# Cross-attention on one core: value products in five passes instead of six, with copies, loads and reciprocals rearranged

## The chip, the cores and the metric

The kernel runs on one core of a Trainium2 chip. The metric is device time in microseconds (us) of one execution; the time before is the median of three runs. The profile is of one further execution, so sums made from it are compared with its own time. Engine names are those of the profile: PE (TensorE), ACT (ScalarE), DVE (VectorE), POOL (GpSimd), SP (the queue that issues nearly all transfers).

## The reference

Only the text part of the attention counts here: the context has 77 rows, so the slices for objects, others and image prompts, which start at row 77, are empty and add nothing.

```python
# x: (32, 512, 640), ctx: (32, 77, 1024), 20 heads of 32 columns
q = heads(x @ to_q_w)
k = heads(ctx @ to_k_w)
v = heads(ctx @ to_v_w)
p = softmax(q @ k^T / sqrt(32))
out = merge(p @ v)
out = out @ to_out_w + to_out_b + x
```

## The kernel before

**Precision.** All products are made from split operands. A float32 value is split into a high part (rounded to the type float32r by a copy, mostly on ACT) and a low part (the value less its high part, mostly on DVE or POOL), and a product of two split operands is three matmuls: high x high, high x low, low x high (`PAIRS`).

**Stages.** First keys and values of all 32 batches are made from the context and written to scratch memory in DRAM (`k_dram`, `v_dram`). Then come 160 *slots*, one for each batch b and each chunk j of 128 columns (four heads): n = 5b + j. The order of every engine's queue is the order in which the program is written (a manual schedule), so each engine works its list in order and waits where an operand is missing.

**A slot n** holds several chunks at different ages:

- `queries(n + 1)` makes the next chunk's queries from the transposed, split x (15 matmuls of 512 columns in two parts, L437); `split_q` splits them (L103, L104).
- `scores(n, t)` for four quarters t: three matmuls of 308 columns (L456) and DVE's maximum per head (L464); `exps(n, t)` exponentiates four heads on ACT and sums them (L474).
- `sums(n - 1)` and `normalize(n - 1, ..)`: reciprocals on DVE (L484), one product on POOL (L489). `transpose_p(n - 1)` turns 32 x 32 blocks on DVE (L496) and writes the probabilities, transposed, to DRAM as 320 rows (10 blocks of 32 keys, three padding keys a head) of 512 queries (L503).
- `load_p` loads an older chunk's rows (L512, L513) into `raw`: 128 rows for each of two pairs of heads in planes 0 and 1, and the other 64 rows in half of plane 2. The probabilities of chunk n - 3 are then split: `cast_p` makes the high parts (ACT, L520), `rest_p` casts the rest rows (ACT, L526) and makes the low parts of planes 0 and 1 (DVE, L527), `last_p` makes the low parts of the rest rows (POOL, L534). The rest rows' high parts lie in partitions 0 to 63 of plane 4 of `pp` and their low parts in partitions 64 to 127.
- `values` multiplies them with the values in `vb` (L548): six matmuls of 512 columns, three for each pair p (high plane, low plane, plane 4), into two PSUM banks `pa`. A value block has its high part in the first 64 columns of a matmul's weights and its low part in the last 64, so high x high is in PSUM's partitions 0 to 63 and the product with the low part in 64 to 127.
- `sum_a` copies partitions 64 to 127 away (ACT, L559) and adds the halves (DVE, L561); `high_a` and `low_a` split the result (ACT L568, DVE L573).
- `piece` does part of the output projection of an earlier batch (L591); `finish` adds residual and bias (DVE, L620) and stores; `add_bias` prepares that sum on POOL (L584).
- For the next batch, `transpose_x` turns x (DVE, L256) in chunks 0 to 2, and `split_x` splits it in the slots of chunks 2 (two splits) and 3 (three): ACT L263, POOL L264.
- `refill` loads the next keys (L418) and values (L426): group 0 holds chunks 0 and 1, group 1 chunks 2 to 4. One half is issued at the start of the slot, the other after `load_p`. Group 1's keys load in chunk 0's slot, group 0's values in chunk 1's, group 0's keys in chunk 2's, group 1's values in chunk 3's.

**The order within a slot**, as far as the change touches it: first half of `refill`, `cast_p`, `high_a` of the chunk taken one slot earlier, `scores(n, 0)`, `rest_p`, `sums`, `last_p`, `normalize`, `low_a`, `exps(n, 0)`, the first queries, `scores(n, 1)`, `load_p`, the second half of `refill`, and so on; `values` and `sum_a` come late in the slot. The tiles `pp` and `pa` exist once each.

Of the kernel before, what the change touches and what calls it, by code (L numbers as in the profile page):

```python
# [23 lines left out]
P = 128  # L24
# [12 lines left out]
    (0, 0, 0, 0, 0, 80),  # L37
    (0, 0, 80, 1, 0, 48),
    (0, 1, 0, 1, 48, 32),
    (0, 1, 64, 1, 48, 32),  # L40
    (1, 0, 48, 3, 0, 80),
    (1, 0, 0, 2, 32, 48),
    (1, 1, 32, 2, 0, 32),
    (1, 1, 96, 2, 0, 32),
]

# [5 lines left out]
def kernel(  # L52
# [340 lines left out]
    raws, pps, ats, pds, sms, pqs, pas, xrs, pos = ({} for _ in range(9))  # L393
# [14 lines left out]
    for g, (j0, nj) in enumerate(GROUPS):  # L408
        vb = main.tile([P, nj, 2, 2, P], FPR, name=f"vb{g}")
        nc.gpsimd.memset(vb.bitcast(F32), 0.0)  # L410
        vbs.append(vb)
# [8 lines left out]
    def load_values(b, g, segments=SEGMENTS):  # L420
        j0, nj = GROUPS[g]
        v = v_dram.rearrange("n i j a d -> n j i (a d)")
        for p, t, r0, i, k0, kn in segments:
            k0 += b * NKEY
            c0 = i % 2 * HD
            nc.sync.dma_start(  # L426
                vbs[g][r0 : r0 + kn, :, p, t, c0 : c0 + 3 * HD].bitcast(F32),
                v[k0 : k0 + kn, j0 : j0 + nj, i, :].bitcast(F32),
            )
# [79 lines left out]
    def load_p(n):  # L509
        pd = pds.pop(n)  # L510
        raw = late[0].tile([P, 3, S], F32, tag="raw", name="raw", bufs=2)
        nc.sync.dma_start(raw[:, 0:2, :], pd.rearrange("(k p) q -> p k q", k=2)[:P])  # L512
        nc.sync.dma_start(raw[:64, 2, :], pd[P : P + 64, :])  # L513
        raws[n] = raw

    def cast_p(n):

        raw = raws[n]
        pp = late[0].tile([P, 5, S], FPR, tag="pp", name="pp", bufs=1)
        nc.scalar.copy(pp[:, 0:2, :], raw[:, 0:2, :])  # L520
        pps[n] = pp

    def rest_p(n):

        raw, pp = raws[n], pps[n]
        nc.scalar.copy(pp[:64, 4, :], raw[:64, 2, :])  # L526
        nc.vector.tensor_tensor(  # L527
            pp[:, 2:4, :], raw[:, 0:2, :], pp[:, 0:2, :].bitcast(F32), ALU.subtract
        )

    def last_p(n):

        raw, pp = raws.pop(n), pps[n]
        nc.gpsimd.tensor_tensor(  # L534
            pp[64:, 4, :], raw[:64, 2, :], pp[:64, 4, :].bitcast(F32), ALU.subtract
        )

    PASSES = [(p, 0, p + c) for p in range(2) for c in (0, 2)] + [(p, 1, 4) for p in range(2)]  # L540

    def values(n):
        b, j = divmod(n, NC_)
        g = GROUP_OF[j]
        pp, vb = pps.pop(n), vbs[g][:, j - GROUPS[g][0]]
        pas[n] = late[1].tile([P, 2, S], F32, tag="pa", name="pa", bufs=1)
        for m, (p, t, c) in enumerate(PASSES):
            nc.tensor.matmul(  # L548
                pas[n][:, p, :],
                vb[:, p, t, :],  # L550
                pp[:, c, :],
                start=(c == p),
                stop=(t == 1),
            )

# [88 lines left out]
    def take(m):  # L644
        values(m)
        sum_a(m)
        high_a(m)
        low_a(m)

    def refill(b, j, part):  # L650

        heads = range(2 * part, 2 * part + 2)
        segments = SEGMENTS[4 * part : 4 * part + 4]
        if j == 0:
            load_keys(b, 1, heads)
        elif j == 1:
            load_values(b, 0, segments)
# [5 lines left out]
    def slot(n, beside=()):  # L663
# [105 lines left out]
    def end():  # L769
# [6 lines left out]
        high_a(N - 4)  # L776
        cast_p(N - 3)
        low_a(N - 4)
# [11 lines left out]
        piece(last - 1, 9)  # L790
        cast_p(N - 2)
# [25 lines left out]
        take(N - 2)  # L817
        cast_p(N - 1)
# [4 lines left out]
        begin(2, 0, 3)  # L823
# [5 lines left out]
        begin(4, 0, 4)  # L829
        begin(5, 0, 4)  # L830
# [78 lines left out]
```

## Time and profile before

| | |
|---|---|
| median of three runs | 1937.06 us (1936.06 to 1937.77) |
| profiled execution | 1935.38 us, span 1933.3 us |
| granted clock of TensorE | 0.998 |
| busy | PE 98%, ACT 79%, DVE 74%, POOL 52% |
| transfers | 431.28 MB, 560919 packets |

A group of the profile names the line, the engine, the operation, output and inputs with their shapes, the count, then the busy time and the mean duration, then the idle time of the engine in front of these instructions and what ended it. A line of the timeline has the start in us from the start of the span, the duration, the engine, the line and the operation; instructions of one kind in a row are merged (x6), and their duration runs from the first start to the last end. Durations of matmuls include the way through the array, so that matmuls in a row overlap; their pitch is less than their duration.

### The profile page before, as it was taken

The numbers are of one execution on the slowest core, as the hardware profiler recorded it, in microseconds if no ns is written. First come the engines' busy times: TensorE is split into PE (matmuls) and PEld (weight loads), VectorE is DVE, ScalarE is ACT, GpSimd is POOL, SyncE is SP. The second block draws the span as 40 slices with busy tenths as digits, with TensorE's granted clock in tenths as the row PEclk, the third lists the DMA queues.
The fourth block names the chain that finished last, engine by engine and source line by source line (L and its number), as shares of the span: only waits on it lengthen the run. The fifth ranks groups of instructions, "written<-read, shape, count | busy, mean of one in ns | idle before, by whom it ended". The sixth has DMA issues, their size and how long they took to land.

```text
span 1933.3 us, 36251 instructions
## 1 busy us (share of the span) xinstructions
PE 1900.7 (98%) x10332; PEld 1696.9 (88%) x10332; DVE 1439.4 (74%) x2334; ACT 1532.6 (79%) x6210; POOL 1013.8 (52%) x668
## 2 busy tenths in 40 slices
PE   9999998999999999999999999999999999999998
PEld 7888896889999999999889998999989998988987
DVE  4444447788888888888788888887888888788875
ACT  3232248888998889888888888889899988888883
POOL 1100054656665566555556555566566656655654
PEclk9999999999999999999999999999999999999999
DMA  9888878888888888888889888888898888888875
GB/s 184 201 196 248 198 195 218 226 229 237 228 224 230 226 227 230 228 241 218 232 230 235 230 224 232 238 232 219 232 238 227 223 228 222 226 227 240 234 198 171
DMA packets 560919, 431.28 MB, mean 223 GB/s; under 512 B 187024, under 2 KB 469072, under 8 KB 560720
## 3 DMA queue, kind: packets, MB, share of 16 engines
q1 hardware_dynamic: 556208, 414.46, 82.8%
q0 software_dynamic: 4416, 14.34, 2.2%
q8 instruction: 84, 1.38, 0.3%
q14 instruction: 115, 0.94, 0.2%
q10 hardware_dynamic: 96, 0.16, 0.0%
HBM read 247.17 MB, written 181.64 MB: 222 GB/s over the span
## 4 chain that ended last, share of the span: by engine, by line
PE 33%; DMA 17%; ACT 16%; DVE 11%; POOL 10%; issue 10%; SPq 3%; DVEq 0%; POOLq 0%; ACTq 0%
PE po L591 8%; PE pq L437 8%; ACT pn L474 7%; DMA raw<-pd 7%; POOL pn L489 7%; PE pv L191 6%; DMA pd<-z 6%; PE pk L191 5%; PE sc L456 4%; POOL pp L534 3%; PE pa L548 3%; ACT xt L263 3%; DVE pp L527 2%; ACT aw L559 2%; DVE nm L464 2%
## 5 line engine op out<-in xcount | busy, mean ns | idle before, releaser
L474 ACT ACTIVATE pn<-sc,nm 128x77 f32<-128x77 f32 x2560 | 800.6, 333 | 65.7 <-DVE nm L464 62.8
L591 PE MATMUL po<-wo_s,at 128*128 128x320 f32 x3840 | 622.8, 310 | 10.2 <-DVE xr L620 6.5
L437 PE MATMUL pq<-xt,wq_s 128*128 128x512 f32 x2400 | 607.2, 393 | 0.6 <-POOL xt L264 0.6
L591 PEld LDWEIGHTS po<-wo_s,at 128*128 128x128 f32 x3840 | 573.9, 188 | 20.1 <-DVE xr L620 17.0
L534 POOL TENSOR_TENSOR pp<-raw,pp 64x512 fp32r<-64x512 f32 x160 | 211.1, 1319 | 647.5 <-ACT pp L526 402.2
L474 ACT ACTIVATION_READ_ACCUMULATOR pn<-sc,nm 128x1 f32 x2560 | 543.7, 212 | 0.0
L437 PEld LDWEIGHTS pq<-xt,wq_s 128*128 128x128 f32 x2400 | 436.9, 188 | 76.8 <-POOL xt L264 1.7
L456 PE MATMUL sc<-kb,qt 128*128 128x308 f32 x1920 | 378.8, 306 | 12.8 <-ACT pn L474 5.9
L456 PEld LDWEIGHTS sc<-kb,qt 128*128 128x128 f32 x1920 | 325.1, 189 | 58.5 <-ACT pn L474 9.4
L489 POOL TENSOR_TENSOR pn<-pn,rs 128x1232 f32<-128x1232 f32 x160 | 364.1, 2276 | 12.6 <-DVE rs L484 0.2
L496 DVE STREAM_TRANSPOSE z<-pn 128x1280 f32<-128x1280 f32 x160 | 241.8, 1512 | 161.1 <-POOL pn L489 152.9
L464 DVE TENSOR_REDUCE nm<-sc 128x4 f32<-128x308 f32 x640 | 295.4, 463 | 54.8 <-PE sc L456 51.6
L527 DVE TENSOR_TENSOR pp<-raw,pp 128x1024 fp32r<-128x1024 f32 x160 | 195.5, 1222 | 82.5 <-ACT pp L520 71.4
L548 PE MATMUL pa<-pp,vb 128*128 128x512 f32 x960 | 252.2, 398 | 1.6 <-DVE pp L527 0.8
L561 DVE TENSOR_TENSOR pa<-pa,aw 64x512 f32<-64x512 f32 x320 | 222.7, 696 | 27.9 <-ACT aw L559 18.7
L559 ACT COPY aw<-pa 64x1024 f32<-64x1024 f32 x160 | 161.8, 1011 | 79.6 <-PE pa L548 77.4
L264 POOL TENSOR_TENSOR xt<-xs,xt 128x512 fp32r<-128x512 f32 x160 | 203.9, 1293 | 38.0 <-ACT xt L263 37.5
L548 PEld LDWEIGHTS pa<-pp,vb 128*128 128x128 f32 x960 | 174.8, 189 | 32.0 <-DVE pp L527 1.1
L584 POOL TENSOR_TENSOR xr<-xr,bias 128x640 f32<-128x640 f32 x128 | 201.3, 1574 | 0.2
L520 ACT CAST pp<-raw 128x1024 fp32r<-128x1024 f32 x160 | 168.8, 1055 | 31.9 <-DMA raw<-pd 31.8
L191 PE MATMUL pk<-ct,wk_s 128*128 128x512 f32 (+1 forms) x600 | 134.5, 382 | 1.4 <-ACT wk_s L103 1.1
L191 PE MATMUL pv<-ct,wv_s 128*128 128x512 f32 (+1 forms) x600 | 133.9, 382 | 0.0
(43 smaller groups left out, 1337.4 us busy)
## 6 DMA issues: line engine op xcount, KB each, us to landing
pd<-z SPq DMA_DIRECT2D x640, 160.0 KB, 3.8
raw<-pd SPq DMA_DIRECT2D x160, 512.0 KB, 4.0
xs<-in_x_dram SPq DMA_DIRECT2D x128, 320.0 KB, 6.2
xr<-in_x_dram SPq DMA_DIRECT2D x128, 320.0 KB, 4.0
out_dram<-xr SPq DMA_DIRECT2D x127, 320.0 KB, 4.0
raw<-pd SPq DMA_DIRECT2D x160, 128.0 KB, 4.2
v_dram<-vs SPq DMA_DIRECT2D x80, 192.0 KB, 4.0
k_dram<-ks POOLq DMA_DIRECT2D x20, 512.0 KB, 4.4
```

The source lines that it names most:

```text
L191: nc.tensor.matmul(held[j][:, :gn], w[:, k, a, :], cts[g, k][:, c, :gn], start=(k == 0 and n == 0), stop=(k == NK - 1 and n == 2),)
L437: nc.tensor.matmul(pqs[n], wq_s[:, k, a, j * P : (j + 1) * P], xts[b, k][:, c, :], start=(k == 0 and m == 0), stop=(k == NC_ - 1 and m == 2),)
L456: nc.tensor.matmul(sc[:, :KCOLS], qt[:, a, t * P : (t + 1) * P], kb[:, j - GROUPS[g][0], c], start=(m == 0), stop=(m == 2),)
L464: nc.vector.tensor_reduce(nm, sc[:, :KCOLS].rearrange("p (h k) -> p h k", k=NKEY), AX.X, ALU.max, negate=True)
L474: nc.scalar.activation(pnb[n % 2][:, at, :NKEY], sc[:, i * NKEY : (i + 1) * NKEY], AF.Exp, bias=nm[:, i : i + 1], accum_out=sms[n][:, at : ...
L489: nc.gpsimd.tensor_tensor(pf, pf, rs.unsqueeze(2).to_broadcast([P, NQ * HPC, NKEY]), ALU.mult)
L496: nc.vector.transpose(z.rearrange("p b t j -> p t b j"), pn.rearrange("p (t h) k -> p t (h k)", t=NQ).rearrange("p t (b i) -> p t b i", i=Q),)
L527: nc.vector.tensor_tensor(pp[:, 2:4, :], raw[:, 0:2, :], pp[:, 0:2, :].bitcast(F32), ALU.subtract)
L534: nc.gpsimd.tensor_tensor(pp[64:, 4, :], raw[:64, 2, :], pp[:64, 4, :].bitcast(F32), ALU.subtract)
L548: nc.tensor.matmul(pas[n][:, p, :], vb[:, p, t, :], pp[:, c, :], start=(c == p), stop=(t == 1),)
L561: nc.vector.tensor_tensor(pa[64 * p : 64 * p + 64, 0], pa[:64, p], aw[:, p], ALU.add)
L591: nc.tensor.matmul(pos[b, t, h][:, :HALF], ats[b * NC_ + j][:, a, t * P : (t + 1) * P], wos[0][:, j, c, h * HALF : (h + 1) * HALF], start= ...
```

## The change

- **Five passes.** The rest rows now lie twice in partitions 96 to 127: planes 0 and 1 hold rows 0 to 127 of each pair of heads, plane 2 the rows 96 to 159 of each (64 rows of either pair, so 32 of each lie in two places). The low parts of planes 0 and 1 are made for 96 partitions only, and the remaining 32 partitions of the two low planes take high parts of the rest rows, copied by POOL from plane 2. So two high passes and two passes over these mixed planes cover all but the low parts of the rest rows, and a fifth matmul, `rest_values`, multiplies those from a tile of their own (`lp`), made by POOL from all 128 partitions of plane 2.
- **Where it runs.** `rest_values` adds into `pa` after `sum_a` has added the halves there, in the next slot, behind the first queries; `high_a` and `low_a` follow behind `scores(n, 1)`.
- **Weights.** `vb` has five blocks per chunk. Three loads for each half of the heads (six, before eight) fill the first four; a new `copy_values` on POOL, in the slots of chunks 1 and 4, copies the rest.
- **Loads.** `load_p` has a second load of 64 rows. Group 0's values now load in chunk 0's slot and group 1's keys in chunk 1's.
- **Order.** One cast on ACT of all three planes; `sums` and `normalize` now stand in front of `rest_p` and `last_p`.

```diff
 SEGMENTS = [
-    (0, 0, 0, 0, 0, 80),
...
+    (0, 0, 0, 0, 80),
+    (0, 80, 1, 0, 48),
+    (2, 96, 1, 48, 32),
+    (1, 0, 2, 0, 80),
+    (1, 80, 3, 0, 48),
+    (3, 96, 3, 48, 32),
 ]
+REST = [(0, 0, 32), (32, 2, 32), (64, 1, 96), (96, 3, 96)]
...
-        vb = main.tile([P, nj, 2, 2, P], FPR, name=f"vb{g}")
+        vb = main.tile([P, nj, 5, P], FPR, name=f"vb{g}")
...
+    def copy_values(g):
+        vb = vbs[g]
+        nc.gpsimd.tensor_copy(vb[:96, :, 2:4, :], vb[:96, :, 0:2, :])
+        for r0, m, c0 in REST:
+            nc.gpsimd.tensor_copy(
+                vb[r0 : r0 + Q, :, 4, c0 : c0 + HD], vb[96:, :, m, HD : 2 * HD]
+            )
...
     def load_p(n):
-        nc.sync.dma_start(raw[:, 0:2, :], pd.rearrange("(k p) q -> p k q", k=2)[:P])
-        nc.sync.dma_start(raw[:64, 2, :], pd[P : P + 64, :])
+        rows = pd[: NBLK * Q].rearrange("(k p) q -> k p q", k=2)
+        nc.sync.dma_start(raw[:, 0:2, :], rows[:, :P].rearrange("k p q -> p k q"))
+        for k in range(2):
+            nc.sync.dma_start(raw[64 * k : 64 * k + 64, 2, :], rows[k, 96:])
...
     def cast_p(n):
-        nc.scalar.copy(pp[:, 0:2, :], raw[:, 0:2, :])
+        nc.scalar.copy(pp[:, 0:3, :], raws[n])
...
     def rest_p(n):
-        nc.scalar.copy(pp[:64, 4, :], raw[:64, 2, :])
         nc.vector.tensor_tensor(
-            pp[:, 2:4, :], raw[:, 0:2, :], pp[:, 0:2, :].bitcast(F32), ALU.subtract
+            pp[:96, 3:5, :], raw[:96, 0:2, :], pp[:96, 0:2, :].bitcast(F32), ALU.subtract
         )
     def last_p(n):
-        nc.gpsimd.tensor_tensor(
-            pp[64:, 4, :], raw[:64, 2, :], pp[:64, 4, :].bitcast(F32), ALU.subtract
-        )
+        nc.gpsimd.tensor_copy(pp[96:, 3, :], pp[32:64, 2, :])
+        nc.gpsimd.tensor_copy(pp[96:, 4, :], pp[96:, 2, :])
+        lp = late[0].tile([P, S], FPR, tag="lp", name="lp", bufs=1)
+        nc.gpsimd.tensor_tensor(lp, raw[:, 2, :], pp[:, 2, :].bitcast(F32), ALU.subtract)
+        lps[n] = lp
     def values(n):
-        for m, (p, t, c) in enumerate(PASSES):
+        for m, c in ((0, 0), (1, 1), (2, 3), (3, 4)):
             nc.tensor.matmul(
-                pas[n][:, p, :], vb[:, p, t, :], pp[:, c, :], start=(c == p), stop=(t == 1),
+                pas[n][:, m % 2, :], vbs[g][:, j - GROUPS[g][0], m, :], pp[:, c, :],
+                start=m < 2, stop=m > 1,
             )
+    def rest_values(n):
+        nc.tensor.matmul(
+            pas[n][:, 0, :], vbs[g][:, j - GROUPS[g][0], 4, :], lps.pop(n),
+            start=False, stop=True, skip_group_check=True,
+        )
...
     def refill(b, j, part):
         if j == 0:
+            load_values(b, 0, segments)
+        elif j == 1:
             load_keys(b, 1, heads)
-        elif j == 1:
-            load_values(b, 0, segments)
...
     def slot(n, beside=()):
             cast_p(taken)
-        if n - 1 in takes:
-            high_a(takes[n - 1])
         s = scores(n, 0)
+        if n:
+            normalize(n - 1, sums(n - 1))
         if taken is not None:
             rest_p(taken)
-        rs = sums(n - 1) if n else None
         if taken is not None:
             last_p(taken)
-        if n:
-            normalize(n - 1, rs)
-        if n - 1 in takes:
-            low_a(takes[n - 1])
+        if j in (1, 4):
+            copy_values(j // 4)
         exps(n, 0, *s)
         if ahead:
             queries(n + 1, 0, 2)
+        if n - 1 in takes:
+            rest_values(takes[n - 1])
         s = scores(n, 1)
+        if n - 1 in takes:
+            taken_parts(takes[n - 1], rest=False)
```

`taken_parts` calls `rest_values` (if asked), `high_a` and `low_a`. The last slots, written out one by one in `end`, get the same calls in the same sense.

More of the change, by code (lines that the diff above doesn't have):

```diff
@@ L391 @@
     late = []
-    raws, pps, ats, pds, sms, pqs, pas, xrs, pos = ({} for _ in range(9))
+    raws, pps, lps, ats, pds, sms, pqs, pas, xrs, pos = ({} for _ in range(10))
     bias = main.tile([P, C], F32, name="bias")
@@ L422, in load_values @@
         v = v_dram.rearrange("n i j a d -> n j i (a d)")
-        for p, t, r0, i, k0, kn in segments:
+        for m, r0, i, k0, kn in segments:
             k0 += b * NKEY
@@ L646, in take, with taken_parts @@
         sum_a(m)
+    def taken_parts(m, rest=True):
+        if rest:
+            rest_values(m)
         high_a(m)
@@ L817, in end @@
         take(N - 2)
+        begin(2, 0, 3)
+        taken_parts(N - 2)
         cast_p(N - 1)
@@ L829, in end @@
         begin(4, 0, 4)
+        taken_parts(N - 1)
         begin(5, 0, 4)
```

36 lines of the change are left out of this document (17 added, 19 removed).

## The prediction

> **What bounds the kernel now.** I read the page's busy times and groups first, then the stretches of five consecutive slots, then the timeline of those slots, the groups with shapes kept apart, the DMA issues and the waits. Page and groups (busy, mean ns of one, idle before):
>
> ```profile
> span 1933.3 us, 36251 instructions
> PE 1900.7 (98%) x10332; PEld 1696.9 (88%) x10332; DVE 1439.4 (74%) x2334; ACT 1532.6 (79%) x6210; POOL 1013.8 (52%) x668
> ...
> L534 POOL TENSOR_TENSOR pp<-raw,pp 64x512 fp32r<-64x512 f32 x160 | 211.1, 1319 | 647.5 <-ACT pp L526 402.2
> L489 POOL TENSOR_TENSOR pn<-pn,rs 128x1232 f32<-128x1232 f32 x160 | 364.1, 2276 | 12.6 <-DVE rs L484 0.2
> L527 DVE TENSOR_TENSOR pp<-raw,pp 128x1024 fp32r<-128x1024 f32 x160 | 195.5, 1222 | 82.5 <-ACT pp L520 71.4
> L264 POOL TENSOR_TENSOR xt<-xs,xt 128x512 fp32r<-128x512 f32 x160 | 203.9, 1293 | 38.0 <-ACT xt L263 37.5
> L584 POOL TENSOR_TENSOR xr<-xr,bias 128x640 f32<-128x640 f32 x128 | 201.3, 1574 | 0.2
> L520 ACT CAST pp<-raw 128x1024 fp32r<-128x1024 f32 x160 | 168.8, 1055 | 31.9 <-DMA raw<-pd 31.8
> ```
>
> PE is busy 98%. The stretches show that this is the bound of each slot: the five lines are chunks 1, 2, 3, 4 of one batch and chunk 0 of the next; columns are length, then PE, PEld, DVE, ACT, POOL busy, clock, DMA share, GB/s.
>
> ```profile
> 990.57:1000.67 10.10, 10.10 (x60) 9.17 (x59) 8.49 (x15) 7.98 (x34) 3.56 (x2) 1.00 0.77 228
> 1000.67:1010.77 10.10, 10.10 (x59) 9.18 (x58) 9.07 (x15) 9.40 (x39) 6.78 (x5) 1.00 0.77 206
> 1010.77:1020.85 10.08, 10.08 (x60) 9.17 (x58) 7.93 (x14) 9.86 (x40) 7.95 (x6) 1.00 0.88 239
> 1020.85:1030.93 10.08, 10.08 (x60) 9.16 (x59) 7.42 (x14) 9.05 (x42) 6.95 (x5) 1.00 0.84 190
> 1030.93:1041.36 10.43, 10.33 (x60) 9.16 (x59) 8.26 (x14) 9.13 (x42) 5.10 (x3) 1.00 1.12 282
> sum 50.79, PE 50.69 PEld 45.84 DVE 41.18 ACT 45.42 POOL 30.34; mean PE 10.14 PEld 9.17 DVE 8.24 ACT 9.08 POOL 6.07
> ```
>
> PE has no gap in four of five slots, at full clock. So a matmul less is worth its full pitch, and whatever makes PE wait is lost for good. The in-order queues of the other engines decide which it is. Their places:
>
> ```profile
> 1001.23 1.05 ACT L520 CAST pp<-raw 128x1024 fp32r<-128x1024 f32 x1
> ...
> 1002.49 0.46 DVE L464 TENSOR_REDUCE nm<-sc 128x4 f32<-128x308 f32 x1
> ...
> 1007.17 1.57 PE L548 MATMUL pa<-pp,vb 128*128 128x512 f32 x6
> ...
> 1011.20 1.55 PE L437 MATMUL pq<-xt,wq_s 128*128 128x512 f32 x6
> ...
> 1011.61 1.05 ACT L520 CAST pp<-raw 128x1024 fp32r<-128x1024 f32 x1
> ...
> 1013.01 2.23 PE L437 MATMUL pq<-xt,wq_s 128*128 128x512 f32 x9
> ...
> 1015.51 1.05 PE L591 MATMUL po<-wo_s,at 128*128 128x320 f32 x6
> ...
> 1016.40 1.55 PE L548 MATMUL pa<-pp,vb 128*128 128x512 f32 x6
> ...
> 1018.90 0.65 DVE L104 TENSOR_TENSOR qt<-pq,qt 128x512 fp32r<-128x512 f32 x1
> 1018.92 3.79 POOL L264 TENSOR_TENSOR xt<-xs,xt 128x512 fp32r<-128x512 f32 x3
> ...
> 1021.91 1.06 ACT L520 CAST pp<-raw 128x1024 fp32r<-128x1024 f32 x1
> ...
> 1027.35 1.56 PE L548 MATMUL pa<-pp,vb 128*128 128x512 f32 x6
> ...
> 1031.49 1.06 ACT L520 CAST pp<-raw 128x1024 fp32r<-128x1024 f32 x1
> ...
> 1032.00 0.46 DVE L464 TENSOR_REDUCE nm<-sc 128x4 f32<-128x308 f32 x1
> ...
> 1039.24 2.27 PE L591 MATMUL po<-wo_s,at 128*128 128x320 f32 x12
> ...
> 1039.84 0.48 DVE L620 TENSOR_TENSOR xr<-po,xr 128x320 f32<-128x320 f32 x1
> ```
>
> **The matmul removed.** Nine matmuls of 512 columns take 2.23 us and six 1.55, so one more costs (2.23 - 1.55)/3 = 0.227 us. Five passes for six: 160 x 0.227 = 36.3 us, 1.13 us a batch. If PE stays the only bound, the profiled execution (1935.4 us, span 1933.3; 1.7 under the median of 1937.1) becomes 1899.
>
> **The rest, engine by engine.**
>
> ```profile
> L526 ACT CAST pp<-raw 64x512 fp32r<-64x512 f32 x160 | 100.2, 626 | 0.0
> ...
> L104 DVE TENSOR_TENSOR qt<-pq,qt 128x512 fp32r<-128x512 f32 x160 | 104.6, 654 | 4.9 <-ACT qt L103 4.9
> ...
> L410 POOL MEMSET vb<- 128x1536 f32 x1 | 1.4, 1381 | 5.3 <-DMA k_dram<-ks 5.3
> ...
> L410 POOL MEMSET vb<- 128x1024 f32 x1 | 1.0, 952 | 0.0
> ```
>
> ACT: one cast of 1536 elements for casts of 1024 and 512. The slope is (1055 - 626)/512 = 0.84 ns, so it takes 1.48 us against 1.68: 0.2 us a slot less on an engine that isn't the bound; nothing. But the low parts (DVE L527) now wait for all 1.48 us, not 1.05.
>
> DVE: the subtract has 96 partitions and still 1024 elements: 1.22 us. The reciprocal only changes place.
>
> POOL: no such copy is in the trace. Below is the memset: slope (1381 - 952)/512 = 0.84 ns, so 0.52 us for 512 elements; above is the subtract L534, 1.32 in the mean. A copy reads one operand, not two, so I take 0.6, nearer the memset. Two a slot, and copy_values twice a batch at some 1.3 us (512 or 768 elements and four short ones). The subtract into the tile lp takes the 1.29 of the xt subtract L264, which has its shape. Per batch POOL goes from 30.3 us to 30.3 + 5 x 1.2 + 2 x 1.3 = 38.9 of 49.7: busier, not full.
>
> DMA: 160 x 128 KB more of raw, 21 of 431 MB; the values save 64 of 384 rows. Shares of 0.77 to 0.88 allow that. Only chunk 0's slot stands at 1.12, and there raw lands later; the next slot has ACT 7.98 busy of 10.10, which covers a cast that starts 1 to 2 us later. I cost it at nothing.
>
> **Moved.** The fifth pass runs one slot later, behind PE's first six query matmuls, and PE's whole queue stands behind it. They start 0.43 into the slot (1011.20), so it comes at 0.43 + 6 x 0.227 = 1.8. It needs lp, which POOL leaves in the slot before, and DVE's sum of the halves, which is done when the maximum of chunk 2's slot starts (1002.49, 1.82 into it), the latest of these: 0.1 there, nothing elsewhere. The high and low parts of a come behind it. In chunk 3's slot PE's projection reads them from 4.74 + 0.23 = 5.0 (high) and 5.3 (low); ACT's high part ends about 2.3 + 1.2 + 0.6 = 4.1, DVE's low part 0.9 to 1.1 behind the low parts of the probabilities: met, if those end by 4.2. The sums reuse one PSUM tile, so the passes also need that low part before 5.9 (6.7 in the other slots): met too. The values of group 0 now load in chunk 0's slot, a slot sooner, and copy_values reads them a slot later; both have a whole slot to land.
>
> **The order on POOL and DVE, on which the sign hangs.** Before, POOL's normalization follows DVE's low parts and never meets them. After, the reciprocal is ahead of the low parts, POOL starts its 2.28 us as soon as that is done, while DVE still waits for the 1.48 us cast. What do they do to each other when they meet? In the first slot with values there is one such meeting, DVE first, with an undisturbed subtract of a later slot below it:
>
> ```profile
> 299.83 1.22 DVE L527 TENSOR_TENSOR pp<-raw,pp 128x1024 fp32r<-128x1024 f32 x1 [1.95 <-ACT pp L520]
> ```
> ```profile
> 300.43 1.75 POOL L534 TENSOR_TENSOR pp<-raw,pp 64x512 fp32r<-64x512 f32 x1 [4.85 <-ACT pp L526]
> ```
> ```profile
> 1013.79 1.29 POOL L534 TENSOR_TENSOR pp<-raw,pp 64x512 fp32r<-64x512 f32 x1 [2.06 <-DMA pd<-z]
> ```
>
> POOL started 0.62 us before DVE's subtract ended and took 1.75 us, not 1.29: it stood still for 0.46 of the 0.62. So POOL doesn't run beside this DVE subtract. Whether DVE stands still when POOL was first, no row shows. The bounds are 0 and the rest of POOL's instruction, up to 2.28 us; nearest is the mirror image just shown, so I take the whole rest. The Trainium skill (SBUF — State Buffer, Who interferes with whom) says that a DVE instruction with two SBUF inputs and a GpSimd one that reads SBUF exclude each other, whoever starts first holding the port for its whole instruction. By that rule the sum is the one below, and for DVE first this trace agrees (1.75 against 1.29).
>
> The sum then goes by slots, in us from each slot's start, slots 0.23 shorter:
> - Chunk 2 (1000.67): the maximum ends at 2.28, the reciprocal at 2.5, the cast at 2.04. DVE is first, 2.45 to 3.67; POOL normalizes to 5.8, copies to 7.0. The passes would start at 6.73 and want the copied rows at 7.19: no stall but the 0.1 above. Then POOL's 1.29, 1.57 and two of 1.29 run to 12.5, 2.6 into the next slot.
> - Chunk 3 (1010.77): cast done at 2.32, POOL holds the port to 2.6, DVE's low parts end at 3.8, normalization at 6.0, copies at 6.6 and 7.2. The passes start at 5.86 here and want the copies at 6.32 and 6.55: PE waits 0.6. POOL ends 3.5 into the next slot.
> - Chunk 4 (1020.85): cast done at 2.54, port free at 3.5, low parts to 4.7, normalization to 6.9, copies to 8.1; wanted at 7.4: PE waits 0.7.
> - Chunk 0 (1030.93): the maximum ends at 1.53, normalization runs 1.85 to 4.13; the cast is done at 2.04, so the low parts run 4.13 to 5.35, 2.5 later than before. DVE's steps behind them (maximum, low a, maximum, transpose, low q, maximum, starting 0.38, 0.55, 0.38, 1.44, 0.57, 0.38 apart) put the end of L620 at 9.45, was 9.39. PE already waits for it there (2.27 for 12 matmuls, 1.92 elsewhere) and comes 0.23 sooner: 0.3 more.
> - Chunk 1: normalization first again, but the cast waits for raw; 0.2 by the same chain.
>
> Together 1.9 - 1.13 = 0.77 us a batch, 31 batches: 24 us. Forecast 1959. With copies of 0.52 the two large stalls shrink to 0.4 each: 1943. If DVE, waiting, also loses the port to POOL's next queued instruction, or the copies take 1.29, the stalls of chunks 3 and 4 grow by some 1.3 together: near 1999.
>
> **Rivals.**
> (a) DVE isn't held by POOL. Then chunk 2 normalizes from 2.5, copies end at 6.0, POOL ends 1.6 into the next slot; there copies end at 5.2 (wanted 6.3), in chunk 4 at 5.5. Only the 0.1 of chunk 2 stays: 1899 + 3 = 1902. It decides if low parts beside the normalization still take 1.22 us. For it: DVE's L104 took 0.65 beside POOL (1018.90), as in the mean; but it reads PSUM and SBUF, L527 SBUF alone. Against: the 1.75.
> (b) The port is held, but copies are at their floor and DVE gets between any two POOL instructions, so that stalls are 0.7 a batch: 1935 - 13 = 1922.
> (c) Keys late. Group 1's keys are now issued in chunk 1's slot, their second half behind one load more.
>
> ```profile
> 1005.72 1.05 SPq L418 DMA_DIRECT2D kb<-k_dram  x2
> ```
> ```profile
> kb<-k_dram SPq DMA_DIRECT2D x128, 57.8 KB, 5.6
> ...
> kb<-k_dram SPq DMA_DIRECT2D x128, 38.5 KB, 3.2
> ```
>
> In chunk 2's slot the second half starts 5.05 after the slot's start, its last issue about 5.6; one more issue, taken at half of this pair's 1.05, makes 6.1. At 3.2 it lands at 9.3, in time for 9.87; at 5.6 it lands at 11.7: 1.8 us a batch, and 1899 + 56 = 1955 without any held port. The 5.6 is measured at the share of 1.12, chunk 1's slot is at 0.77: unlikely.
> (d) DVE starves through POOL's whole run of queued instructions (2.28 + 1.2 + 1.29 us): the low parts end 2.5 later than in the forecast's slots, ACT has some 1 us of slack a slot, so over 1.5 us x 155 more: above 2150.
>
> **Numbers.** Forecast case 0.48, (a) 0.32, (b) 0.08, (c) 0.07, (d) 0.05. Under 0.2% (about what a measurement of this kernel can tell) is no change; 0.04 of the first and 0.02 of (c) fall there. Faster 0.32 + 0.08 = 0.40, same 0.06, slower 0.54. The likeliest case's own range is 1943 to 1999; to hold (a) with the bounds of its terms and the long copies the range goes from 1895 to 2002.
>
> **What would show it.** 800 passes of 0.227 pitch. L527 at 1.22 or, beside the normalization, at up to 3.4 us (or starting later): that alone tells the forecast from (a). POOL copies at 0.52 to 1.29. PE's idle time in front of the third and fourth pass, put down to POOL copies, some 40 us in all; if it's under 10 us and slots are 9.85 long, I'm wrong. PE's wait for keys at chunk 2 tells (c).

## The result and the profile after

The changed kernel takes 2003.42 us (median of four runs, 2000.84 to 2004.45) against 1937.02 for the kernel before on the same chip: ratio 1.0341, 95% interval 1.0323 to 1.0359. It is slower by 66 us; the forecast was 22 slower, with a range that ended at 2002.

From the profile after: busy times, then the groups that answer to L489, L527 and L534 of before (busy, mean ns of one, idle time ahead), and last, from the full list of groups, the second copy. The new copies are L542 and L543, the subtract into `lp` is L545, the normalization is L497 and DVE's low parts are L535.

```profile
span 2002.3 us, 36798 instructions
PE 1896.2 (95%) x10172; PEld 1668.2 (83%) x10172; DVE 1596.7 (80%) x2334; ACT 1525.0 (76%) x6050; POOL 1448.0 (72%) x1308
...
L497 POOL TENSOR_TENSOR pn<-pn,rs 128x1232 f32<-128x1232 f32 x160 | 387.7, 2423 | 242.2 <-DVE rs L492 155.8
L535 DVE TENSOR_TENSOR pp<-raw,pp 96x1024 fp32r<-96x1024 f32 x160 | 355.8, 2224 | 140.2 <-ACT pp L529 134.0
L542 POOL CAST pp<-pp 32x512 fp32r<-32x512 f32 x160 | 211.0, 1319 | 18.9 <-ACT pp L529 8.4
L545 POOL TENSOR_TENSOR lp<-raw,pp 128x512 fp32r<-128x512 f32 x160 | 207.0, 1294 | 12.9
```
```profile
L543 POOL CAST pp<-pp 32x512 fp32r<-32x512 f32 x160 | 99.0, 619 | 9.5
```

PE has 160 matmuls less (10172 for 10332) and is busy 95% of a longer span. The low parts on DVE went from 1222 to 2224 ns with the same 1024 elements a partition. The second copy takes 619 ns in the mean (L543); L542, a copy of the same shape one place earlier, takes 1319.

The stretches of one batch, chunks 1, 2, 3, 4 and the next chunk 0 (columns as before: length, then PE, PEld, DVE, ACT, POOL busy, clock, DMA share, GB/s):

```profile
1127.99:1138.90 10.91, 10.30 (x59) 8.91 (x57) 9.73 (x15) 8.88 (x39) 7.15 (x9) 1.00 0.82 216
1138.90:1148.88 9.98, 9.98 (x57) 8.98 (x58) 9.14 (x16) 9.12 (x37) 7.41 (x6) 1.00 0.78 228
1148.88:1160.13 11.25, 10.11 (x58) 8.97 (x57) 9.14 (x13) 9.30 (x38) 11.04 (x9) 1.00 0.89 242
1160.13:1169.99 9.86, 9.86 (x59) 8.98 (x58) 8.62 (x13) 8.72 (x37) 9.45 (x11) 1.00 0.80 197
1169.99:1180.72 10.73, 10.10 (x59) 8.90 (x57) 9.89 (x15) 9.22 (x42) 8.89 (x7) 1.00 1.01 273
sum 52.73, PE 50.35 PEld 44.73 DVE 46.52 ACT 45.24 POOL 43.95; mean PE 10.07 PEld 8.95 DVE 9.30 ACT 9.05 POOL 8.79
```

Only chunk 4's slot reaches the 9.85 of a PE without gaps. Chunk 3's slot (the third line) lost most. Its timelines, POOL, DVE and PE (last column: idle time and what ended it):

```profile
1148.55 2.55 POOL L263 TENSOR_TENSOR xt<-xs,xt 128x512 fp32r<-128x512 f32 x2
1151.05 2.28 POOL L497 TENSOR_TENSOR pn<-pn,rs 128x1232 f32<-128x1232 f32 x1
1153.39 1.49 POOL L542 CAST pp<-pp 32x512 fp32r<-32x512 f32 x1
1154.94 0.61 POOL L543 CAST pp<-pp 32x512 fp32r<-32x512 f32 x1
```
```profile
1149.89 0.24 DVE L492 RECIPROCAL rs<-sm 128x16 f32<-128x16 f32 x1
1151.23 3.17 DVE L535 TENSOR_TENSOR pp<-raw,pp 96x1024 fp32r<-96x1024 f32 x1 [1.10 <-ACT pp L529]
1154.33 0.46 DVE L472 TENSOR_REDUCE nm<-sc 128x4 f32<-128x308 f32 x1
1154.72 0.67 DVE L592 TENSOR_TENSOR at<-pa,at 128x512 fp32r<-128x512 f32 x1
```
```profile
1155.45 0.86 PE L610 MATMUL po<-wo_s,at 128*128 128x320 f32 x4 [1.14 <-DVE at L592]
```

POOL ends its x split and takes the normalization at once; DVE's subtract is ready 0.18 us later and stands until 1153.33, when the normalization ends; it is done 1.07 us after that, where the whole subtract alone takes 1.22. In that time DVE has the port, and the copy queued on POOL takes 1.49 for 0.61. The same holds in all 127 slots of this trace in which the subtract began beside a POOL instruction (126 times the normalization): it ended 1.07 to 1.09 us after that instruction's end. Behind the subtract stand a maximum and the low part of `a` (L592), and PE's projection (L610) waits 1.14 us for that.

### The profile page after: what moved, and what is told of

It is laid out like the page before. It is cut to its first block, busy times and chain, and to the rows that moved or that the text cites. A ratio compares the mean times of both kernels' runs of the same rounds, so it can differ in the third digit from the quotient of the medians.

```text
span 2002.3 us, 36798 instructions
## 1 busy us (share of the span) xinstructions
PE 1896.2 (95%) x10172; PEld 1668.2 (83%) x10172; DVE 1596.7 (80%) x2334; ACT 1525.0 (76%) x6050; POOL 1448.0 (72%) x1308
## 3 DMA queue, kind: packets, MB, share of 16 engines
q8 instruction: 82, 1.34, 0.3%
## 4 chain that ended last, share of the span: by engine, by line
PE 30%; DMA 21%; ACT 20%; issue 12%; DVE 10%; SPq 5%; POOL 2%; DVEq 0%; ACTq 0%; POOLq 0%
PE pq L445 9%; ACT pn L482 8%; DMA raw<-pd 8%; DMA xs<-in_x_dram 8%; PE po L610 7%; ACT pp L529 6%; PE pv L190 4%; PE sc L464 4%; PE pk L190 4%; SPq L511 3%; ACT aw L578 3%; DMA pd<-z 3%; DVE z L504 3%; DVE nm L472 3%; ACT xt L262 2%
## 5 line engine op out<-in xcount | busy, mean ns | idle before, releaser
L610 PE MATMUL po<-wo_s,at 128*128 128x320 f32 x3840 | 640.5, 312 | 54.3 <-DVE at L592 28.4
L610 PEld LDWEIGHTS po<-wo_s,at 128*128 128x128 f32 x3840 | 576.0, 188 | 79.8 <-DVE xr L639 41.8
L497 POOL TENSOR_TENSOR pn<-pn,rs 128x1232 f32<-128x1232 f32 x160 | 387.7, 2423 | 242.2 <-DVE rs L492 155.8
L535 DVE TENSOR_TENSOR pp<-raw,pp 96x1024 fp32r<-96x1024 f32 x160 | 355.8, 2224 | 140.2 <-ACT pp L529 134.0
L529 ACT CAST pp<-raw 128x1536 fp32r<-128x1536 f32 x160 | 237.5, 1484 | 30.2 <-DMA raw<-pd 27.7
L542 POOL CAST pp<-pp 32x512 fp32r<-32x512 f32 x160 | 211.0, 1319 | 18.9 <-ACT pp L529 8.4
L545 POOL TENSOR_TENSOR lp<-raw,pp 128x512 fp32r<-128x512 f32 x160 | 207.0, 1294 | 12.9
L554 PE MATMUL pa<-pp,vb 128*128 128x512 f32 x640 | 176.9, 397 | 3.9 <-DVE at L592 2.1
L211 POOL DMA_DIRECT2D k_dram<-ks x20 | 14.5, 727 | 190.0 <-DVE ks L103 190.0
```

The lines of the kernel that those rows point to most:

```text
L497: nc.gpsimd.tensor_tensor(pf, pf, rs.unsqueeze(2).to_broadcast([P, NQ * HPC, NKEY]), ALU.mult)
L529: nc.scalar.copy(pp[:, 0:3, :], raws[n])
L535: nc.vector.tensor_tensor(pp[:96, 3:5, :], raw[:96, 0:2, :], pp[:96, 0:2, :].bitcast(F32), ALU.subtract)
L610: nc.tensor.matmul(pos[b, t, h][:, :HALF], ats[b * NC_ + j][:, a, t * P : (t + 1) * P], wos[0][:, j, c, h * HALF : (h + 1) * HALF], start= ...
```

## The experiments

The slots of most kernels in one table: mean length in us by chunk, from the starts of each slot's first scores matmul (27 batches in the middle of the trace), with the median time and the ratio to the kernel before, run beside it on the same chip (1934.44 to 1938.23 us, by chip). e3, e11, e17 and e18 leave something out of the result, as their expectations say.

| run | 1 | 2 | 3 | 4 | 0 | us | ratio, interval |
|---|---|---|---|---|---|---|---|
| before | 10.08 | 10.11 | 10.07 | 10.08 | 10.61 | 1937 | 1 |
| after | 10.98 | 10.25 | 11.05 | 9.85 | 10.75 | 2003.42 | 1.0341 (1.0323-1.0359) |
| e1 | 10.71 | 10.11 | 10.52 | 10.30 | 11.56 | 2010.01 | 1.0385 (1.0368-1.0403) |
| e16 | 11.96 | 10.70 | 10.07 | 10.08 | 10.57 | 2005.76 | 1.0359 (1.0333-1.0385) |
| e2 | 10.66 | 10.27 | 10.39 | 11.03 | 14.41 | 2124.74 | 1.098 (1.0964-1.0997) |
| e3 | 11.02 | 10.28 | 10.43 | 9.85 | 10.74 | 1985.70 | 1.0256 (1.0236-1.0275) |
| e4 | 10.31 | 10.65 | 11.28 | 9.85 | 10.73 | 2000.74 | 1.0340 (1.0325-1.0356) |
| e18 | 10.32 | 10.59 | 11.26 | 9.85 | 10.73 | 2000.06 | 1.0339 (1.0321-1.0356) |
| e5 | 10.72 | 10.52 | 9.87 | 9.85 | 12.46 | 2010.27 | 1.0388 (1.0365-1.0410) |
| e6 | 9.99 | 11.38 | 9.87 | 9.85 | 12.05 | 2010.71 | 1.0370 (1.0346-1.0393) |
| e8 | 10.88 | 10.06 | 10.31 | 10.45 | 10.24 | 1977.76 | 1.0218 (1.0188-1.0248) |
| e9 | 10.27 | 10.47 | 10.50 | 10.50 | 9.85 | 1965.89 | 1.0158 (1.0139-1.0177) |
| e10 | 9.93 | 10.22 | 11.05 | 10.76 | 10.02 | 1973.96 | 1.0191 (1.0176-1.0206) |
| e11 | 11.56 | 10.00 | 9.87 | 9.85 | 10.30 | 1968.34 | 1.0172 (1.0155-1.0189) |
| e17 | 11.05 | 10.02 | 9.87 | 9.85 | 10.39 | 1949.40 | 1.0072 (1.0053-1.0092) |

Theory H was the forecast's: POOL's normalization holds DVE's subtract. The expectations name three others: W (POOL's added work costs the time), K (keys come late) and D (in chunk 0's slot the DMA engines have too much to move, so `raw` comes late for chunk 1).

**e1: the order alone, in the kernel before.**

```diff
         s = scores(n, 0)
+        if n:
+            normalize(n - 1, sums(n - 1))
         if taken is not None:
             rest_p(taken)
-        rs = sums(n - 1) if n else None
         if taken is not None:
             last_p(taken)
-        if n:
-            normalize(n - 1, rs)
```

> The kernel before with one part of the change alone: reciprocals and normalization in front of the low parts of the probabilities; six passes, no copies, no new loads. Theory H (DVE's subtract is held while POOL normalizes): the subtract, 1.22 us before, grows to 2 to 3 us in most slots, the low part of a and all behind it come 1 to 2 us later, PE waits for them, and the time rises to 1955 to 1985 us. Rival W (the loss comes from POOL's added copies and POOL's load): the order alone costs nothing, 1937 +- 5 us, and the subtract stays below 1.5 us in the mean.

Measured 74 us slower; H had the sign and the longer subtract, but only 19 to 49 us. The group in e1:

```profile
L527 DVE TENSOR_TENSOR pp<-raw,pp 128x1024 fp32r<-128x1024 f32 x160 | 411.7, 2573 | 64.8 <-ACT pp L520 64.8
```

2573 ns for 1222, with six passes, the old loads and no copy. So the order alone lengthens the subtract, and PE waits in chunks 0 and 1 for the sum with `xr` and in 0, 3 and 4 for the low part of `a`.

**e2: the change with the old order.** Reciprocal, low parts, POOL's three instructions, and the normalization last.

```diff
-        if n:
-            normalize(n - 1, sums(n - 1))
         if taken is not None:
             rest_p(taken)
+        rs = sums(n - 1) if n else None
         if taken is not None:
             last_p(taken)
+        if n:
+            normalize(n - 1, rs)
```

> The changed kernel with the normalization put back behind the low parts and POOL's three instructions for the rest rows; everything else of the change stays. Theory H: the subtract falls from a mean of 2.22 us to 1.2 to 1.6 us, PE's wait for the low part of a in chunk 3's slot (L592, 65 us in the changed kernel with the weight loads) goes; in its place the normalization and the transpose behind it come some 1 us later than in the kernel before; 1920 to 1965 us. Rival W: POOL has the same work, so the time stays within 10 us of 2003.

Both theories missed. The subtract is back at 1233 ns, but POOL's copies wait for the cast and then for the subtract (the first takes 1573 ns), the normalization for the copies, and DVE's transposition for that. From the waits of e2:

```profile
DVE z L504 <- POOL pn L497: 253.0, 114, 2.9
```

With POOL's added work, normalizing late is worse than normalizing first: DVE's queue behind the transposition holds PE, and chunk 0's slot is 3.7 us longer than in after.

**e3: the change without the two copies.**

```diff
-            pp[:96, 3:5, :], raw[:96, 0:2, :], pp[:96, 0:2, :].bitcast(F32), ALU.subtract
+            pp[:, 3:5, :], raw[:, 0:2, :], pp[:, 0:2, :].bitcast(F32), ALU.subtract
...
-        nc.gpsimd.tensor_copy(pp[96:, 3, :], pp[32:64, 2, :])
-        nc.gpsimd.tensor_copy(pp[96:, 4, :], pp[96:, 2, :])
```

> The changed kernel without POOL's two copies of the rest rows' high parts (the products of these rows with the low parts of the values are left out); the low parts are made for 128 partitions instead, in the same number of elements. Theory H: the subtract is held as before and nothing that PE waits for depends on the copies; 1990 to 2003 us. Rival W, and the step of the prediction that had PE wait for the copies: 1940 to 1970 us.

1985.70, between the two: the copies cost about 17 us (1.0341 - 1.0256 of 1937), all of it in chunk 3's slot (11.05 to 10.43). In after PE waited only a few us in all for the copies themselves. They cost by pushing an x split into chunk 3's slot, ahead of the normalization: there, by the medians of the timelines, the normalization ran from 2.18 to 4.45 us of the slot in after and from 1.34 to 3.62 here, DVE's subtract ended at 4.69 instead of 5.53, and the low part of `a` at 5.68 instead of 6.51.

**e4: all keys of group 1 at the start of chunk 1's slot.**

```diff
-            load_keys(b, 1, heads)
+            load_keys(b, 1, range(4 - 4 * part))
```

> The changed kernel with all four heads' keys of group 1 issued at the start of chunk 1's slot instead of half of them behind the load of the probabilities. Theory K (late keys are a part of the loss): the waits in front of chunk 2's first scores (0.7 to 1.0 us a batch in the changed kernel, a third of it put down to keys) go, 12 to 30 us less: 1973 to 1991 us. Theory H alone, with those waits coming from late sums and exponentials: within 5 us of 2003.

Chunk 1's slot falls by 0.67, chunks 2 and 3 give back 0.63; the time stays (1.0340), as H alone had it. Keys were waited for, but they were not what the batch ended on.

**e5: low parts first, then copies, normalization, and the subtract into `lp` last; e6: e5 with the keys of e4 and, in chunk 0's slot, the sum with `xr` ahead of the last maximum.**

```diff
     def last_p(n):
-        raw, pp = raws.pop(n), pps[n]
+        pp = pps[n]
         nc.gpsimd.tensor_copy(pp[96:, 3, :], pp[32:64, 2, :])
         nc.gpsimd.tensor_copy(pp[96:, 4, :], pp[96:, 2, :])
+    def last_l(n):
+        raw, pp = raws.pop(n), pps[n]
         lp = late[0].tile([P, S], FPR, tag="lp", name="lp", bufs=1)
...
-        if n:
-            normalize(n - 1, sums(n - 1))
         if taken is not None:
             rest_p(taken)
+        rs = sums(n - 1) if n else None
         if taken is not None:
             last_p(taken)
+        if n:
+            normalize(n - 1, rs)
+        if taken is not None:
+            last_l(taken)
```

The early sum with `xr`, in e6 alone:

```diff
+        if has_out and j == 0:
+            finish()
         if has_out:
             s = scores(n, 3)
```

> The changed kernel with another order: low parts of the probabilities, then reciprocals on DVE; POOL's two copies, then the normalization, then the subtract into lp. Theory H: the subtract is no longer held by the normalization (mean 1.2 to 1.5 us), the normalization starts 1.3 us sooner than with all three instructions in front of it (2125 us), and the transposes behind it come in time in most slots; 1905 to 1950 us. Rival W (POOL's work as such costs the time, wherever it stands): above 1990 us.

> The order of e5, with two waits of PE taken away that stand in both kernels or in the changed one: in chunk 0's slot the sum with the residual (which PE waits for before it can open the next bank) ahead of the last maximum, and all heads' keys of group 1 at the start of chunk 1's slot. Theory H and the pitch of a matmul: with no wait left but small ones, 31 x 49.3 us and the ends, 1885 to 1915 us, under the kernel before. If POOL's added work is what limits, 1950 us or more.

Both of H's forecasts missed by 60 us or more; W's held (above 1990, and 1950 or more). Chunks 3 and 4 are ideal, but in chunks 4 and 0 the normalization runs from 6.1 to 8.5 us of the slot, and chunk 0's slot takes 12.46. With this much work on POOL no tried order frees both the subtract and the transposition.

**e7: the kernel before with that early sum.**

> The kernel before with the same early sum with the residual in chunk 0's slot alone, as the base for e6. PE's wait there is 0.36 us in most batches and up to 1.2: 1920 to 1930 us if it goes; 1937 if the maximum that then comes later takes its place.

1934.21, ratio 0.998 (0.9969 to 0.9991), not the 1920 to 1930 hoped for. It is the only version below before, by an amount at the edge of what can be told.

**e8, e10: the normalization in two or four instructions; e9: two, with the keys and the early sum (as has e10).**

```diff
-        pf = pnb[n % 2][:, :, :NKEY]
-        nc.gpsimd.tensor_tensor(
-            pf, pf, rs.unsqueeze(2).to_broadcast([P, NQ * HPC, NKEY]), ALU.mult
-        )
+        half = NQ * HPC // 2
+        for i in range(2):
+            pf = pnb[n % 2][:, i * half : (i + 1) * half, :NKEY]
+            nc.gpsimd.tensor_tensor(pf, pf, ..., ALU.mult)
```

> The changed kernel with the normalization as two instructions of half the columns each; nothing else. Theory H with the port held for one instruction at a time: the waiting subtract gets in between the halves, its mean falls from 2.22 to some 1.6 us, the low part of a comes about 1 us sooner in the slots of chunks 0, 3 and 4, PE's wait in chunk 3's slot goes: 1955 to 1985 us. If DVE and POOL only share a bandwidth, or DVE waits until POOL's queue is empty, nothing changes: 2003 +- 5 us (a little more for one more instruction).

> The kernel after with the normalization as two instructions, all keys of group 1 at the start of chunk 1's slot, and in chunk 0's slot the sum with xr ahead of the last maximum. Theory H (with the port free after half an instruction, what is left of the stalls is small waits that these two edits address: keys 0.33 and xr in chunk 0 0.30 us a batch): 1955 to 1972, chunk 0 and chunk 2 slots 0.2 to 0.4 shorter than with halves alone (10.24 and 10.06). Rival W (POOL's added work hands the waits on to the next slot, as it did in the earlier run of these two edits): 1974 to 1985, the same sum of slots in another distribution.

> The same with the normalization as four instructions of about 0.6 us. Theory H (what DVE's subtract loses is the rest of the one POOL instruction that runs): median of the subtract 1.3 to 1.5 us, maximum under 1.9, and 5 to 20 us less than with halves. Rival W (POOL's own time decides; four instructions cost it some 0.2 us more a slot and DVE gets in more often, so copies end later): same as halves or up to 15 us slower, with PE's wait for copies before chunk 4's third pass growing over 0.6 us a batch.

Halves alone give back some 25 us, as H had it. From e8's timelines, one subtract and its normalization, in a slot of chunk 3:

```profile
1134.89 2.23 DVE L540 TENSOR_TENSOR pp<-raw,pp 96x1024 fp32r<-96x1024 f32 x1 [1.12 <-ACT pp L534]
```
```profile
1134.82 3.39 POOL L499 TENSOR_TENSOR pn<-pn,rs 128x616 f32<-128x616 f32 x2
```

With shorter instructions DVE gets in: the subtract starts 0.07 us after the first half, which undisturbed takes 1.23, and ends 1.07 us after that half would; the second half waits, and the pair takes 3.39 for some 2.45. The subtracts have a median of 1.50. Quarters gave no more (median 1.45; 8 us slower than e9, as W had it): now POOL is late, and PE waits 1.07 us a batch in chunk 3's slot for the copies. That is the wait that the forecast had seen. e9, 1.0158, is within H's range and the best five-pass version that leaves nothing out; but of its two edits only chunk 0's slot gained (10.24 to 9.85), while chunk 2's grew (10.06 to 10.47).

**e11: two memsets of the same tile in place of the normalization.** POOL is as long busy in the same place, but reads nothing.

```diff
-        nc.gpsimd.tensor_tensor(
-            pf, pf, rs.unsqueeze(2).to_broadcast([P, NQ * HPC, NKEY]), ALU.mult
-        )
+        for _ in range(2):
+            nc.gpsimd.memset(pf, 0.0125)
```

> The kernel after, where the normalization is replaced by two memsets of the same tile, about 2.26 us on POOL in the same place, so that POOL is as long busy but reads nothing (the probabilities become a constant: normalization is left out). Theory H (the port, not POOL's time, is the main cause): DVE's subtract at 1.15 to 1.25 us beside the memsets, chunk 3's wait for the low part gone, and 1900 to 1945, that is most of the 66 us. Rival W (POOL's time alone delays the transposition and the copies): subtract short, yet 1960 to 2003. If writing alone holds the port too, the subtract stays at 2.2 in the mean and the time at 1995 to 2010.

```profile
L498 POOL MEMSET pn<- 128x1232 f32 x320 | 367.1, 1147 | 205.6 <-ACT pn L482 114.4 <-issue 77.9
L534 DVE TENSOR_TENSOR pp<-raw,pp 96x1024 fp32r<-96x1024 f32 x160 | 193.4, 1209 | 158.2 <-ACT pp L528 119.6 <-DMA pd<-z 38.6
```

POOL's 2.29 us a slot are still there and the subtract takes 1209 ns: it is POOL's reading that holds DVE, not its time. In 126 slots the subtract began while a memset ran. The Trainium skill (SBUF — State Buffer, Who interferes with whom) says that such a DVE instruction collides with a GpSimd one that reads SBUF, not with one that only writes it; these two rows agree. Yet the time was W's: chunks 3 and 4 are ideal, 33 us come back, and chunk 1's slot grows to 11.56, where ACT's cast waits for `raw` and starts 2.33 us into the slot at the median (1.47 in after, 1.00 in before). A third cause stands there.

**e12 to e15: two loads of x later.** They were moved from the end of chunk 4's slot to behind the load of `raw`: in after, with the memsets, in e9, and in e7.

```diff
-        if n == NC_:
+        if j == 0 and b and b + 1 < B:
             load_x(b + 1, (2, 3))
...
-        if j == 4 and b + 2 < B:
-            load_x(b + 2, (0, 1) if not b else (2, 3))
+        if j == 4 and not b and b + 2 < B:
+            load_x(b + 2, (0, 1))
```

> The kernel after; the loads of the quarters 2 and 3 of x, which every batch issues at the end of chunk 4's slot, moved into chunk 0's slot behind the load of raw. Theory D (a third cause besides the port and POOL's queue: in chunk 0's slot the DMA engines are over full, the third load of raw and the values now stand there, so raw lands 1 to 2 us into chunk 1's slot and delays the cast): raw's cast in chunk 1 starts by 1.0 us at the median instead of 1.6, chunk 1's slot falls from 10.98 to 10.2-10.6, time 1980 to 1995. Rival H alone (chunk 1's waits come from POOL and DVE): chunk 1's slot within 0.1, time 1998 to 2006.

> The kernel after with two memsets in place of the normalization (normalization is left out) and the same two loads of x later. There chunk 1's slot took 11.56 us and raw's cast started at 2.39. Theory D: cast by 1.2, chunk 1's slot 10.0 to 10.5, per batch 50.0 to 50.6, time 1915 to 1940. Rival (POOL's copies or the sum with xr, not raw, make the wait): chunk 1's slot stays above 11, time 1960 to 1972.

> The kernel after with the normalization in two instructions, the sum with xr and the keys earlier, and the same two loads of x later. Theory D with H: the waits of chunks 1 and 2 (0.43 and 0.6 us a batch) shrink by half, the waits for copies and low parts of chunks 3 and 4 (1.25) stay: 1945 to 1960. Rival: 1962 to 1972 as without it.

> The kernel before with the sum with xr earlier in chunk 0 and the same two loads of x later. Before has little to win there (chunk 1's slot is 10.08, PE full). Theory D: raw lands sooner, but nothing waited for it: 1931 to 1936, equal to the earlier run without the moved loads (1934) within 3. If the move disturbs another queue: 1938 to 1950.

All missed: 2127.34, 2090.08, 2101.29 and 2015.87 (ratios 1.0992, 1.0796, 1.0865, 1.0414). `raw` did land sooner (in e13 0.2 us into chunk 1's slot instead of 2.2), but DVE's transpositions then waited for x and chunk 1's slot took 12.6 to 16.0 us. These runs say nothing on D.

**e16: the DMA part alone, in the kernel before.**

```diff
         nc.sync.dma_start(raw[:64, 2, :], pd[P : P + 64, :])
+        nc.sync.dma_start(raw[64:, 2, :], pd[96 : P + 32, :])
...
         if j == 0:
-            load_keys(b, 1, heads)
-        elif j == 1:
             load_values(b, 0, segments)
+        elif j == 1:
+            load_keys(b, 1, heads)
```

> The kernel before with only the DMA part of the change: a second load of 64 rows into the unused half of raw's third part (128 KB more a slot), the values of group 0 loaded in chunk 0's slot and the keys of group 1 in chunk 1's. Theory D (the DMA engines are over full in chunk 0's slot, raw lands later for chunk 1): raw's cast in chunk 1 0.5 to 1.5 us later, slots of chunks 1 and 2 longer, 1945 to 1965. Rival (DMA costs nothing, as the forecast had it): 1934 to 1940.

71 us slower, beyond D's own 8 to 28. `raw`'s cast in chunk 1 does come later, by 0.7 us at the median, as D had it, but most of the loss comes another way. SP's queue tells how; first chunk 0's slot of before (start 1030.93), then of e16 (1067.35), issues only:

```profile
1035.11 0.44 SPq L512 DMA_DIRECT2D raw<-pd  x1
1035.60 0.54 SPq L513 DMA_DIRECT2D raw<-pd  x1
1036.19 1.85 SPq L418 DMA_DIRECT2D kb<-k_dram  x2
1038.88 2.40 SPq L503 DMA_DIRECT2D pd<-z  x4
```
```profile
1073.06 0.38 SPq L512 DMA_DIRECT2D raw<-pd  x1
1074.02 0.45 SPq L513 DMA_DIRECT2D raw<-pd  x1
1075.41 0.45 SPq L514 DMA_DIRECT2D raw<-pd  x1
1076.21 1.75 SPq L426 DMA_DIRECT2D vb<-v_dram  x4
1078.06 2.46 SPq L503 DMA_DIRECT2D pd<-z  x4
```

SP's own waits in e16:

```profile
SPq L512 <- DMA pd<-z: 170.0, 178, 3.7
...
SPq L513 <- DMA xs<-in_x_dram: 19.7, 29, 1.3
SPq L514 <- DMA xs<-in_x_dram: 19.3, 29, 1.2
```

Eight loads of values stand where four of keys stood, and a third load of `raw`. SP waits between them for older transfers to land, so `pd` is written from 10.71 us of the slot instead of 7.95 (medians 11.4 and 8.3). The next loads of `raw`, in chunk 1's slot, wait for that, and behind them, in the same queue, stands the second half of the keys. PE, at the start of chunk 2's slot, and 2.8 us later:

```profile
1089.94 0.66 PE L456 MATMUL sc<-kb,qt 128*128 128x308 f32 x3 [1.91 <-DMA kb<-k_dram]
...
1093.21 2.85 PE L437 MATMUL pq<-xt,wq_s 128*128 128x512 f32 x9
```
```profile
1089.94:1101.69 11.75, 11.75 (x58) 10.48 (x59) 7.87 (x14) 8.12 (x33) 7.47 (x5) 0.85 0.87 249
```

The wait has a second price. Nine query matmuls take 2.85 us here, where they take 2.23 in before, and the granted clock of this slot is 0.85: for 3.4 us it was 0.5. This came in ten of 29 batches, each time after a wait of PE of 1.83 us or more (of 13 such waits; none of the shorter ones brought it). Chunk 2's slot took 11.72 us there and 10.18 in the others, so some 15 of the 71 us come in this way. The slow clock is also in e2 and e12 to e15, whose times hold more than their waits.

e16 is not quite the change's own part: the kernel before needs eight loads of values, where the change makes six. In after `pd` is written from 9.8 us of chunk 0's slot, at the median, between the two.

**e17 and e18: one store less in chunk 0's slot**, with the memsets and in after.

```diff
-            elif h == 1:
+            elif h == 1 and (t != 1 or b == B - 1):
                 nc.sync.dma_start(out[b, t * P : (t + 1) * P, :], xr)
```

> The kernel after with two memsets in place of the normalization (normalization left out), and without the store of the second quarter of each batch's rows, the one that is issued in chunk 0's slot ahead of raw (128 of 512 rows are left out of the output; 328 KB a batch). Nothing else moves. Theory D: raw's cast in chunk 1 about 1 us sooner than 2.39, chunk 1's slot 10.2 to 11.0 instead of 11.56, 1925 to 1955. Rival (the wait comes from POOL and DVE): 1962 to 1972.

> The kernel after without that store (128 of 512 rows are left out of the output). Theory D with H: chunks 1 and 2 lose half of their added 1.0 us a batch, the other slots stay: 1980 to 1995. Rival (port and POOL alone): 1999 to 2006.

e17: 19 us less than e11, and chunk 1's slot 11.05 for 11.56, about as D had it. e18: nothing (1.0339 for 1.0341); chunk 1's slot loses 0.66, chunks 2 and 3 give 0.55 back. Once the port is free, DMA traffic decides a part of the time; while the port is held, it is hidden. This store is in before too: the change's own loads were not taken out of the changed kernel.

## Why the prediction was wrong, point by point

**What held.** The sign, and the mechanism that it hung on: L535 took up to 3.18 us beside the normalization (forecast up to 3.4), which tells it from rival (a). The copy's price was 0.61 against 0.6, `lp` came out as costed (1.29), and the matmul was worth its 1.13 us a batch: chunk 4's slot is 9.85, 0.23 shorter than before. `copy_values` was put too low: 1.5 us in chunk 1's slot and 1.9 in chunk 4's, for some 1.3. Rival (d) falls: where the subtract waited, it got the port before the copy queued behind the normalization (L542 at 1.49).

**The stalls.** Against the slots of before less 0.23 the change added, by the table, 1.13 in chunk 1 (forecast 0.2), 0.37 in 2 (0.1), 1.21 in 3 (0.6), 0.00 in 4 (0.7) and 0.37 in 0 (0.3): 3.08 us for 1.9. Less 1.13 that is 1.95 for 0.77 a batch. In the profiled executions 145 slots from the tenth on took 55.9 us more, everything ahead of them 7.7, the rest 5.4: the 69.0 between the spans. The 7.7 were not in the forecast, which counted whole batches alone. Ahead of the tenth slot the clock was at 0.5 for 20.5 us in after and for 6.8 in before, which is worth 6.8 us at most; e1 and e16 are 6.1 and 6.8 us longer there. What starts it was not taken apart.

**The step that failed most: "Chunk 3 (1010.77): cast done at 2.32, POOL holds the port to 2.6, DVE's low parts end at 3.8".** The cast did end at 2.32, but POOL's x splits ended at 2.2, and the normalization was first by about 0.2 us. DVE's low parts ended at 5.5, not 3.8, and PE waited at the projection for the low part of `a`, 1.2 us, not at the passes for the copies, 0.6. The forecast had checked that reader ("met, if those end by 4.2") and did not ask what follows if the order at the port turns round. In chunk 4's slot the same walk of POOL's backlog erred the other way: there it ended at 2.1, not 3.5, because chunk 3's slot had become longer and gave POOL the time.

**"DMA: ... I cost it at nothing."** Wrong as a statement on its own: e16 shows nearly this part alone, with two loads more, to cost 71 us in the kernel before, by the route of rival (c), which had put the keys' second half at 6.1 plus one latency by the issue times of chunk 2's slot of before. In chunk 1's slot SP reaches it later (the last issue at 8.4 us in e16 and 7.0 in after, medians), since the load of `raw` ahead of it waits for late writes of `pd`. In the changed kernel as it stands, earlier keys (e4) or less traffic (e18) won about nothing, because what chunk 1 wins chunks 2 and 3 give back.

**Why the parts don't add.** Order alone +74, DMA part alone +71, one pass less -36 (the forecast's estimate): 109, without POOL's added work; measured +66. Our reading, which e4 and e18 support but no run shows as a whole: a slot waits for whichever chain is last (DVE's, POOL's or the DMA's), and a stall gives the others time. Taken away one by one from the changed kernel, by the ratios: the read on the port 33 us (e11), the copies 17 (e3), one store's traffic 0 (e18), and 19 once the port is free (e17). What holds e17 15 us above before was not settled; in its trace PE waits 16.7 us for keys, 11.6 for the sum with `xr` and 10.5 for exponentials, more than half of it in chunk 1's slot (11.05).

## What to carry to other kernels

Before an instruction is moved ahead on a second engine, ask not only whether it is free earlier but what it shares with the engine it passes: a 2.28 us normalization that met no one cost 74 us one place earlier. Where two queues meet at a port or a slot's end within 0.2 us, price both orders and follow each to its last reader. And try the parts of a change alone as well as left out: of parts that cost 66 us together, one cost 74 alone and one, nearly alone, 71, and yet relieving the second in the changed kernel gave nothing.

## What the hardware showed that was not expected

- Port in both directions: DVE's subtract 1.15 to 3.18 us beside POOL's normalization; POOL's copy 0.61 to 1.67 and halves of the normalization, 1.23 alone, to 2.28 beside DVE's subtract. Memsets beside it: 1.21. The engine that waits gets the port at the end of the other's running instruction: in after, e1 and e8 the subtract ended 1.07 to 1.15 us after the end of the POOL instruction beside which it began, in each of 380 meetings. Where POOL had a copy queued (L542), the subtract went ahead of it. So the length of one instruction, not of the queue, sets the price.
- After a wait of PE of 1.83 us or more the granted clock fell to 0.5 for 3.4 us in ten of e16's 13 cases, and nine matmuls took 2.85 us for 2.23.
- In none of the traces of before, after and e16 were more than seven of SP's transfers still under way when it issued the next (422 of after's issues found seven): a full queue of large loads of x delays issues of small ones. Whether the chip or the program's semaphores set that limit, no run tells.
